# Deformable sampling in tiles of 6 by 16 pixels for 2 by 12 positions, with the corners out of reach gathered apart

## The chip, the core and the metric

The kernel runs on one core of one Trainium2 chip. The metric is device time in microseconds (us) of one execution; a kernel's time is the median of its runs. TensorE (PE in the profile, its weight loads PEld) multiplies matrices, VectorE (DVE) and ScalarE (ACT) work elementwise and carry results out of TensorE's accumulators, GpSimd (POOL) does small leftovers, SyncE (SP) issues most DMAs. Each engine works through its own instructions in order and waits on semaphores of the others.

## The reference

Two images of 256 channels and 128 by 128 pixels pass two layers. Layer 0 normalises by groups, runs three branches (dilation 1, 9, 12) of a deformable depthwise 3 by 3 convolution, and then a 1 by 1 convolution, three layer norms over channels and an MLP. Layer 1 is a group norm and a plain 3 by 3 convolution with quantised weights. What the change touches is the deformable part: each pixel and tap has its own offset, computed by a convolution, and the sample is bilinear between four corners.

```python
def _bilinear(x, py, px):
    y0, x0 = jnp.floor(py), jnp.floor(px)
    for dy in (0.0, 1.0):
        for dx in (0.0, 1.0):
            yc, xc = y0 + dy, x0 + dx
            wgt = (1.0 - jnp.abs(py - yc)) * (1.0 - jnp.abs(px - xc))
            valid = (yc >= 0) & (yc < H) & (xc >= 0) & (xc < W)
            ...
            out = out + g * (wgt * valid)[:, None]

def _branch(x, w_off, w_def, lw, lb, pad, dil):
    off = _conv(x, w_off, pad, dil)
    y = _deform_dw(x, off, w_def, pad, dil)
    return jax.nn.gelu(_ln2d(y, lw, lb), approximate=False)
...
x1 = _branch(x, off_w1, def_w1, bw1, bb1, 1, 1)
x2 = _branch(x, off_w2, def_w2, bw2, bb2, 9, 9)
x3 = _branch(x, off_w3, def_w3, bw3, bb3, 12, 12)
out = _ln2d(x1 + x2 + x3 + c, n1_w, n1_b)
h = gelu(h @ mlp_w1.T + mlp_b1) @ mlp_w2.T + mlp_b2
```

## The kernel before

**Phase A** (`phase_a`, once an image) normalises the image, writes it pixel by pixel into a table in DRAM (`table`, 256 channels a row), computes the offsets (`offsets`, eight image rows a call) and turns them into hat functions (`make_hats`): for each tap and each row or column of a tile, the weight `min(|distance|, 1) - 1` of every output pixel. They go to DRAM (`hats`). `offsets` keeps the largest absolute offset of its rows in `amax` (L381). After phase A the maximum over all of them goes through GpSimd into a flag (L512 to L518), and the program branches on it: above REACH, the general path `sample_any` gathers every corner; else `sample_near` runs, as it does here.

**The sampling stage** (`sample_near`) never gathers. A tile of the table, TR by TC = 8 by 16 pixels, lies on the 128 partitions (`xs`, L764). It serves RI by CI = 2 by 10 base positions, with a reach of 3 pixels on each side. For a unit (image, row of tiles, branch) `build` (L816) multiplies the row hats `hy` with the column hats `hx` into `A`, the bilinear weights of every pixel of a tile for every position and tap. A matmul of the tile with `A` (L889) is then the sampling of 2 x 10 positions x 9 taps = 180 columns; 14 tiles cover a row. ScalarE copies the result into `ev` (L898, three buffers); VectorE adds it, tap by tap, into a ring of image rows per branch (`accumulate`, L867; the first tap by ScalarE, L860). This is done for each of two channel halves: I call one unit's one half a c-step. There are 67 rows of tiles an image, so a row of tiles makes six c-steps and a group of four image rows twelve.

**The tail** (`Tail`) is the rest of layer 0, written as generators that `advance` steps along: at the head of each c-step, once in its middle, and elsewhere. `normalised` (L576) is a layer norm over channels: transposes of the pixels (L593) into PSUM, a copy to `T` (L595), statistics on VectorE (L603, L605), scale on ScalarE (L614), transposes back (L626). `branch` runs it on the ring's finished rows for each branch and group; `finish` adds the 1 by 1 convolution, the MLP and two more norms (L573, L682, L686, L720, L741). A branch's norm begins LAG = 5 advances after its rows are done.

The order on every engine in this stage is that of the program text, since the instructions are pinned (`pin`). In a c-step it is: the tail's pieces, the matmuls and copies (with the tail's middle piece), then, in the second half, `prepare(u + 2)`, which builds the unit after the next and so needs this unit's `A` free, and loads hats; then `accumulate`. `A` has two buffers, so the builds of a c-step stand on VectorE between its matmuls and its accumulation.

**Phase C** is layer 1's convolution.

Of the kernel before, what the change touches and what calls it, by code (L numbers as in the profile page):

```python
# [9 lines left out]
F32 = mybir.dt.float32  # L10
I32 = mybir.dt.int32
U32 = mybir.dt.uint32
BF16 = mybir.dt.bfloat16
# [6 lines left out]
P = 128  # L20
# [18 lines left out]

REACH = 3  # L40
LIMIT = float(REACH)
RI, CI = 2, 10
TR, TC = RI + 2 * REACH, CI + 2 * REACH
NT = -(-(W + 2 * REACH) // CI)
WT = NT * CI + 2 * REACH
AO = 12
WA = 28 + W
NH = TR + TC
HALF = 64
# [6 lines left out]
LAG = 5  # L56
XCLS = (0, 1, 2, 8, 9)
NPAT = RI + len(XCLS) + 1

# [8 lines left out]
def conv_preact_kernel(ctx: ExitStack, tc: tile.TileContext, t: dict, out: bass.AP):  # L68
# [66 lines left out]

    table = dram("table", [HT * WT, C])

    HY = H + 3
    hats = dram("hats", [NOFF // 6, TR + TC, HY, 3, W])
    offd = dram("offd", [H, W, NOFF])  # L140
    g12d = dram("g12d", [C, HW])
# [33 lines left out]
    gn1 = []  # L175
    amax = const.tile([P, NB * (H // ZG)], F32, name="amax")

# [99 lines left out]
    def phase_a(b, pool, psum, k, beside):  # L277
# [53 lines left out]
        def offsets(G):  # L331
# [37 lines left out]
            for br, dil in enumerate(DILS):  # L369
# [9 lines left out]
            nc.vector.tensor_copy(offs.rearrange("p r n -> p (r n)"), po[:, 0 : ZG * NOFF])  # L379
            i = b * (H // ZG) + G  # L380
            nc.vector.tensor_reduce(  # L381
                amax[:, i : i + 1],
                offs.rearrange("p r n -> p (r n)"),
                AX.X,
                ALU.max,
                apply_absolute_value=True,
            )
            nc.sync.dma_start(
# [3 lines left out]
            parts = k["parts"][G % 2]  # L392
            rest = pool.tile([P, ZG, NOFF], F32, name="rest", tag="rest", bufs=2)
            first, second = parts[:, 0, :, 0:NOFF], parts[:, 0, :, HALF : HALF + NOFF]
# [55 lines left out]
    with ExitStack() as actx:  # L450
        psum = actx.enter_context(tc.tile_pool(name="ps_a", bufs=1, space=PSUM))

        def gps():
# [7 lines left out]
            "wz": ap.tile([P, KC, NZ], F32, name="wz"),  # L461
            "shift": ap.tile([P, len(dxs), P], F32, name="shift"),
            "hatw": ap.tile([P, 2, NTAP * NH], BF16, name="hatw"),
            "parts": [ap.tile([P, 2, ZG, P], BF16, name=f"parts{i}") for i in range(2)],
# [8 lines left out]
        for b in range(NB):  # L473
            stats = ap.tile([P, KC, NGRP, 6], F32, name=f"stats1_{b}", tag=f"stats1_{b}")
            for c in range(KC):
                for g0 in range(0, NGRP, XT):
                    xt = ap.tile([P, XT * NG], F32, name="xt", tag="xt", bufs=3)
                    nc.sync.dma_start(
                        xt,
                        x[b, c * P : (c + 1) * P].rearrange("p h w -> p (h w)")[  # L480
                            :, g0 * NG : (g0 + XT) * NG
                        ],
                    )
                    for j in range(XT):
                        nc.vector.bn_stats(stats[:, c, g0 + j, :], xt[:, j * NG : (j + 1) * NG])
            if b == 0:
                load_now()
                nc.sync.dma_start(k["wz"], t["wz"].rearrange("(k p) n -> p k n", p=P))
                nc.sync.dma_start(k["shift"], t["shift"])
                hatw = ap.tile([P, 2, NTAP * NH], F32, name="hatw32", tag="xt", bufs=3)  # L490
                nc.sync.dma_start(hatw, t["hatw"])
                nc.vector.tensor_copy(k["hatw"], hatw)
                pattern = ap.tile([P, NG], F32, name="pattern", tag="xt", bufs=3)
                nc.sync.dma_start(pattern[HALF : HALF + NPAT], t["pattern"])
                for pl in k["planes"]:
                    nc.vector.tensor_copy(
                        pl[HALF : HALF + NPAT, 1, :], pattern[HALF : HALF + NPAT]
                    )
            mean, rstd = group_norm(stats, f"gn1_{b}", gps)
            gn1.append((mean, rstd))  # L500

            nc.vector.tensor_scalar(negmean[b], mean, -1.0, None, ALU.mult)
            for c in range(KC):
                nc.vector.tensor_scalar(
                    convs[b][:, c, :], convs[b][:, c, :], rstd[:, c : c + 1], None, ALU.mult
                )
            phase_a(b, ap, psum, k, beside)
# [3 lines left out]

    far = small.tile([P, 1], F32, name="far", tag="far")  # L512
    nc.vector.tensor_reduce(far, amax, AX.X, ALU.max)
    farall = small.tile([P, 1], F32, name="farall", tag="farall")
    nc.gpsimd.partition_all_reduce(farall, far, P, bass.bass_isa.ReduceOp.max)
    flag = const.tile([P, 1], I32, name="flag")
    nc.vector.tensor_scalar(flag, farall, LIMIT, None, ALU.is_gt)
    beyond = nc.values_load(flag[0:1, 0:1], min_val=0, max_val=1)  # L518
    same = nc.values_load(eq[0:1, 0:1], min_val=0, max_val=1)

# [4 lines left out]
    class Tail:  # L525
# [3 lines left out]

        def __init__(self, pool, psum, pin):  # L530
            self.pool, self.psum, self.pin = pool, psum, pin
            self.waiting, self.running = deque(), []
            self.now = self.last = self.norms = 0
            self.read = set()
# [41 lines left out]
        def normalised(self, z, src, what=None):  # L576
# [8 lines left out]
            T = self.tile("T")  # L585
            Tv = T.rearrange("p k n -> p (k n)").rearrange("p (j c) -> p j c", c=C)
            for h in range(NB4 // 2):
                tp = self.bank("tp")
                for j in range(2):
                    for c in range(KC):  # L590
                        i = j * KC + c
                        px = slice((2 * h + j) * P, (2 * h + j + 1) * P)
                        pin(nc.tensor.transpose(tp[:, i * P : (i + 1) * P], src[:, c, px], ident))  # L593
                pin(
                    nc.scalar.copy(  # L595
                        Tv[:, 2 * h : 2 * h + 2, :].rearrange("p j c -> p (j c)"), tp
                    )
                )
# [153 lines left out]
    def sample_near(pool, psum, k):  # L752

        pin = tc.keep_in_program_order
        tail = Tail(pool, psum, pin)
        units = [(b, Rt, br) for b in range(NB) for Rt in range(NR) for br in BRS]
# [3 lines left out]
        def load_tiles(b, Rt):  # L760

            xts[b, Rt] = []
            for T in range(NT):
                xt = pool.tile([P, C], F32, name="xs", tag="xs", bufs=20)  # L764
                src = bass.AP(
                    table[b].tensor,
                    table[b].offset + (Rt * RI * WT + T * CI) * C,
                    [[C, TC], [WT * C, TR], [1, C]],
                )
                nc.sync.dma_start(xt, src)  # L770
                xts[b, Rt].append(xt)
# [10 lines left out]
        def load_hats(u):  # L782
            b, Rt, br = units[u]
            for ky in taps(u):
                i0, i1 = valid(Rt, br, ky)
                hq = hats[b][br * 3 + ky + 1]
                y0 = Rt * RI - REACH - ky * DILS[br] + i0
                hy = pool.tile([P, RI, 3, W], F32, name="hy", tag="hy", bufs=3)
                hx = pool.tile([P, RI, 3, W], F32, name="hx", tag="hx", bufs=3)
                pitch = HY * 3 * W  # L790
# [78 lines left out]
        def sample(u, c):  # L869
# [13 lines left out]
            for T in range(0, NT, 2):  # L883
                if T // 2 == NT // 4:
                    tail.advance()
                pm = psum.tile([P, 2, 256], F32, name="pm", tag="pm", bufs=4)
                for j in range(2):
                    pin(
# [9 lines left out]
                    nc.scalar.copy(  # L898
                        ev[:, m0:m1, T * CI : (T + 2) * CI].rearrange(
                            "p m (t j) -> p t m j", j=CI  # L900
                        ),
                        pm[:, :, 0:n].rearrange("p t (m j) -> p t m j", j=CI),
                    )
# [36 lines left out]
    def sample_any(b, pool, psum):  # L940
        xbase = pool.tile([P, NTAP], F32, name="xbase", tag="xbase", bufs=1)
        nc.sync.dma_start(xbase, t["xbase"])
        dw = pool.tile([P, NTAP, C], F32, name="dw", tag="dw", bufs=1)
        nc.sync.dma_start(dw, t["defwt"].partition_broadcast(P))
        with tc.For_i(0, H, 1) as y:
            of = pool.tile([P, NOFF], F32, name="of", tag="of", bufs=1)
            nc.sync.dma_start(of, offd[b][bass.ds(y, 1)].rearrange("a w n -> w (a n)"))
            yb = pool.tile([P, NTAP], F32, name="yb", tag="yb", bufs=1)
            nc.sync.dma_start(
# [8 lines left out]
            for c, src in ((0, yb), (1, xbase)):  # L958
                nc.vector.tensor_tensor(
                    pos[:, c * NTAP : (c + 1) * NTAP].rearrange("p (b k) -> p b k", k=9),  # L960
                    ov[:, c],
                    src.rearrange("p (b k) -> p b k", k=9),
                    ALU.add,
# [13 lines left out]
            for dy, wy in ((0, om), (1, pos)):  # L977
                for dx, wx in ((0, om), (1, pos)):
# [5 lines left out]
                        xi, fl[:, NTAP : 2 * NTAP],  # L984
                        float((2 * REACH + dy) * WT + 2 * REACH + dx), None, ALU.add,
                    )
# [5 lines left out]
            for tap in range(NTAP):  # L992
                s = pool.tile([P, C], F32, name="s", tag="s", bufs=2)
                for j in range(4):
# [4 lines left out]
                        out_offset=None,  # L999
                        in_=table[b],  # L1000
                        in_offset=bass.IndirectOffsetOnAxis(ap=at[:, i : i + 1], axis=0),
# [33 lines left out]
    with cmp.Else():  # L1035
        with ExitStack() as bctx:
            psum = bctx.enter_context(tc.tile_pool(name="ps_b", bufs=1, space=PSUM))
            pool = bctx.enter_context(tc.tile_pool(name="bpool", bufs=1))
            k = {
                "A": [pool.tile([P, 9, RI, WA], F32, name=f"A{i}") for i in range(2)],  # L1040
            }
# [276 lines left out]
```

## Time and profile before

| what | us |
|---|---|
| median of three runs (7613.6 to 7631.05) | 7616.63 |
| the profiled execution, its own time | 7634.92 |
| its span in the profile | 7633.1 |
| TensorE busy | 7040.9 (92%) |
| VectorE busy | 6109.5 (80%) |
| ScalarE busy | 4832.0 (63%) |
| GpSimd busy | 712.8 (9%) |

Phase A ends at about 934 us, the first tiles of the sampling stage are asked for at 941.6, and phase C begins at about 6590. Inside the sampling stage each image starts with about ten rows of tiles without much tail work. An f32 matmul is recorded as two matmul instructions; a transpose or a bf16 matmul as one. The busy share of an engine is over the whole span; what sets the pace of the sampling stage is to be read from that stage alone, and from where one engine stands in its program relative to another.

### The profile page before, as it was taken

Reading aid. Unit: us, or ns where it says so; the run is one execution under the profiler, and the core shown is the slowest. Engines: PE = TensorE matmul, PEld = TensorE weight load, DVE = VectorE, ACT = ScalarE, POOL = GpSimd, SP = SyncE. Lnnn points to the kernel's source line nnn. Section 1 sums busy time; section 2 is a strip of 40 time slices with the busy share of each in tenths; the row PEclk is TensorE's granted clock in tenths of the full one; section 3 lists DMA queues with packets and bytes.
Section 4 is the critical chain, followed back from the end, with each engine's and each line's share of the span. In section 5 each row is a group of like instructions: output and inputs, shape, how many; then the busy total and the mean of one; then the engine's idle time right before and its main releaser. Section 6 shows DMA issues by size and latency. Waiting matters only on the chain. (4 is left out here: it accounts for less than half of the span.)

```text
span 7633.1 us, 114421 instructions
## 1 busy us (share of the span) xinstructions
PE 7040.9 (92%) x37984; PEld 5353.3 (70%) x37984; DVE 6109.5 (80%) x12723; ACT 4832.0 (63%) x10150; POOL 712.8 (9%) x1292
## 2 busy tenths in 40 slices
PE   6899888999999999999988999999999999899999
PEld 3555487777887788887777877887888777444444
DVE  7756557888888888988578888888888986677675
ACT  2344366777777777777676777777777777433232
POOL 0000000111111111111100111111111111000000
PEclk9999989999999999999999999999999999899999
DMA  8866689999999999998699999999999995222121
GB/s 285 265 193 197 181 231 250 248 253 256 256 255 252 254 259 255 258 256 231 180 239 246 254 255 253 256 254 253 251 259 254 254 252 161 90 75 76 69 78 47
DMA packets 856311, 1658.87 MB, mean 217 GB/s; under 512 B 116704, under 2 KB 403216, under 8 KB 851480
## 3 DMA queue, kind: packets, MB, share of 16 engines
q1 hardware_dynamic: 838296, 1617.84, 78.1%
q10 hardware_dynamic: 17408, 33.56, 1.3%
q8 instruction: 304, 4.98, 0.3%
q14 instruction: 303, 2.48, 0.1%
HBM read 1381.02 MB, written 270.06 MB: 216 GB/s over the span
## 5 line engine op out<-in xcount | busy, mean ns | idle before, releaser
L889 PE MATMUL pm<-A,xs 128*128 128x180 f32 (+2 forms) x22288 | 3624.6, 318 | 355.6 <-ACT ev L898 248.8
L889 PEld LDWEIGHTS pm<-A,xs 128*128 128x128 f32 x22288 | 3400.5, 195 | 598.0 <-ACT ev L898 347.0
L867 DVE SCALAR_TENSOR_TENSOR ring<-ev,defw,ring 128x256 f32<-128x256 f32 (+3 forms) x6344 | 2780.4, 459 | 339.1 <-ACT ev L898 159.0
L898 ACT COPY ev<-pm 128x360 f32<-128x360 f32 (+2 forms) x5572 | 2244.9, 449 | 791.3 <-PE pm L889 483.3
L816 DVE TENSOR_TENSOR A<-hy,hx 128x768 f32<-128x768 f32 x1130 | 1026.1, 947 | 413.1 <-DMA hx<-hats 300.6
L1172 PE MATMUL pc<-cring,signs 128*128 128x512 bf16 x4608 | 1005.3, 381 | 20.0 <-ACT cring L1119 13.3
L1172 PEld LDWEIGHTS <-signs 128*128 128x128 bf16 x4608 | 452.0, 98 | 572.8 <-issue 27.0
L614 ACT ACTIVATE T<-T,rs 128x256 f32<-128x256 f32 x1280 | 661.9, 589 | 180.5 <-POOL rs L610 180.4
L607 POOL TENSOR_SCALAR rs<-mv 128x4 f32<-128x4 f32 x320 | 122.8, 384 | 4904.3 <-DVE mv L605 2681.5
L573 PE MATMUL hp<-T,w 128*128 128x512 f32 x1024 | 503.8, 617 | 12.9 <-ACT T L692 12.9
L603 DVE BATCH_NORM_STATS2 st<-T 128x6 f32<-128x256 f32 x1280 | 447.0, 412 | 25.3 <-ACT T L595 25.2
L320 PE MATMUL pz<-wz,xa 128*128 128x486 f32 x1024 | 463.7, 582 | 3.1 <-DVE zr L327 3.1
L573 PE MATMUL h<-hT,w 128*128 128x512 f32 x1024 | 460.1, 592 | 0.0
L642 ACT ACTIVATE T<-zc,bb,bw 128x512 f32<-128x512 f32 x384 | 277.5, 773 | 228.0 <-PE zc L626 227.9
L860 ACT ACTIVATE ring<-ev,defw 128x256 f32<-128x256 f32 (+1 forms) x788 | 392.2, 503 | 24.1
L1180 ACT ACTIVATE o<-xl,l1b 128x1024 f32<-128x1024 f32 x64 | 73.5, 1148 | 501.8 <-DMA out_x<-o 394.8
L626 PEld LDWEIGHTS zc<-ident,T 128*128 128x128 f32 x2560 | 315.0, 147 | 96.3 <-issue 61.9
L626 PE MATMUL zc<-ident,T 128*128 128x128 f32 x2560 | 358.7, 284 | 19.7 <-ACT T L614 13.8
L595 ACT COPY T<-tp 128x512 f32<-128x512 f32 x640 | 340.5, 583 | 42.5 <-PE tp L593 42.3
L609 POOL TENSOR_TENSOR rs<-rs,mhalf 128x4 f32<-128x4 f32 x320 | 365.0, 1141 | 0.0
L1119 ACT CAST cring<-D 128x2048 bf16<-128x2048 f32 (+1 forms) x140 | 245.0, 1755 | 183.4 <-PE pc L1172 125.1
L573 PEld LDWEIGHTS h<-hT,w 128*128 128x128 f32 x1024 | 189.1, 190 | 186.6 <-issue 186.1
(118 smaller groups left out, 5226.4 us busy)
## 6 DMA issues: line engine op xcount, KB each, us to landing
hy<-hats SPq DMA_DIRECT2D x1114, 384.0 KB
hx<-hats SPq DMA_DIRECT2D x1114, 384.0 KB
xs<-table SPq DMA_DIRECT2D x1876, 128.0 KB
g12d<-T SPq DMA_DIRECT2D x128, 512.0 KB
other<-g12d SPq DMA_DIRECT2D x128, 512.0 KB
hats<-hb SPq DMA_DIRECT2D x64, 720.0 KB
hats<-hb SPq DMA_DIRECT2D x64, 576.0 KB
xl<-x1d SPq DMA_DIRECT2D x56, 640.0 KB
```

The lines of the kernel that those rows point to most:

```text
L320: nc.tensor.matmul(pz[:, 0:NZ], lhsT=xt[:, c, r, :], rhs=k["wz"][:, c, :], start=c == 0, stop=c == KC - 1,)
L573: nc.tensor.matmul(out, lhsT=w, rhs=v, start=i == 0, stop=i == n - 1)
L603: pin(nc.vector.bn_stats(st[:, j, :], Tv[:, j, :]))
L609: nc.gpsimd.tensor_tensor(rs[:, 0, :], rs[:, 0, :], mhalf[:, 0:NB4], ALU.pow)
L614: nc.scalar.activation(Tv[:, j, :], Tv[:, j, :], AF.Identity, scale=rs[:, 0, j : j + 1], bias=rs[:, 1, j : j + 1],)
L626: nc.tensor.transpose(zc[:, j * P : (j + 1) * P], Tv[:, j, c * P : (c + 1) * P], ident)
L816: nc.vector.tensor_tensor(dst, hy[:, i0:i1].rearrange("p i t w -> p t i w"), hx[:, i0:i1].rearrange("p i t w -> p t i w"), ALU.mult,)
L860: pin(nc.scalar.mul(dst, src, w))
L867: pin(nc.vector.scalar_tensor_tensor(dst, src, w, dst, ALU.mult, ALU.add))
L889: nc.tensor.matmul(pm[:, j, 0:n], lhsT=xts[b, Rt][T + j][:, c * P : (c + 1) * P], rhs=A[:, m0:m1, AO + (T + j) * CI : AO + (T + j + 1) * C ...
L898: nc.scalar.copy(ev[:, m0:m1, T * CI : (T + 2) * CI].rearrange("p m (t j) -> p t m j", j=CI), pm[:, :, 0:n].rearrange("p t (m j) -> p t m ...
L1172: nc.tensor.matmul(pc[:, bank, :], lhsT=w[:, m * P : (m + 1) * P], rhs=xc[:, i, k, t * JC : (t + 1) * JC, kx : kx + W], start=j == 0, stop ...
```

## The change

The reach falls from 3 pixels to 2, and tiles of 6 by 16 pixels (96 partitions) serve 2 by 12 positions. Eleven tiles cover a row, a matmul has 216 columns, and there are 66 rows of tiles an image. `xs` has 18 buffers for 20. Hats keep their number of rows in DRAM.

`offsets` no longer keeps one maximum: for every pixel it keeps, per component, the largest distance of an offset from the middle of its tile's reach (`reach`). After phase A, `missing` lists the pixels where that is over what a tile covers, up to 42 of them, by counting and small matmuls, reads their offsets and base positions back with indirect DMAs, and works out for up to two taps a pixel the weights and table rows of the corners that no tile has. `lacking` gathers those rows and sums them into `extra` [126, 3 branches, 256 channels], each value split into three bf16 parts on three partitions. The flag now says that the lists overflow.

In the tail, `normalised`, when called from `branch`, makes a selection matrix `S` on VectorE (1 where a list entry's pixel is a column's pixel) and adds `S` times `extra` to the transposes in PSUM, with two bf16 matmuls a bank.

```diff
-REACH = 3
-LIMIT = float(REACH)
-RI, CI = 2, 10
+REACH = 2
+RI, CI = 2, 12
...
+PX = TR * TC
...
+SLOTS = 42
+ROWS = 3 * SLOTS
+EACH = 2
...
-            nc.vector.tensor_reduce(
-                amax[:, i : i + 1],
-                offs.rearrange("p r n -> p (r n)"),
-                AX.X,
-                ALU.max,
-                apply_absolute_value=True,
-            )
+            rest = pool.tile([P, ZG, NOFF], F32, name="rest", tag="rest", bufs=2)
+            nc.vector.tensor_tensor(rest, offs, k["mid"], ALU.subtract)
+            planes = rest.rearrange("p r (b c k) -> p c r b k", c=2, k=9)
+            for comp in range(2):
+                nc.vector.tensor_reduce(
+                    reach[:, comp, b * H + G * ZG : b * H + (G + 1) * ZG],
+                    planes[:, comp], AX.XY, ALU.max, apply_absolute_value=True,
+                )
...
+    def missing(psum, pool):
...
+        nc.vector.tensor_scalar(V, reach[:, 0], SPAN[0], None, ALU.is_gt)
+        nc.vector.scalar_tensor_tensor(V, reach[:, 1], SPAN[1], V, ALU.is_gt, ALU.max)
+        nc.vector.tensor_reduce(cnt, V, AX.X, ALU.add)
...
+        gather(of, offs_all, 0)
+        gather(base[:, 0], t["ybase"], 1)
+        gather(base[:, 1], t["xbase"], 2)
...
+    def lacking(pool, m):
...
+                m["gather"](G, tables, i, m["idx"][:, j])
...
+        miss = missing(ps_m, mpool)
+    extra, ids = lacking(mpool, miss), miss["ids"]
     farall = small.tile([P, 1], F32, name="farall", tag="farall")
-    nc.gpsimd.partition_all_reduce(farall, far, P, bass.bass_isa.ReduceOp.max)
+    nc.gpsimd.partition_all_reduce(farall, miss["worst"], P, bass.bass_isa.ReduceOp.max)
...
+            add = what is not None and self.offs is not None
+            if add:
+                b, br, g = what
+                S = pool.tile([ROWS, NG], BF16, name="S", tag="S", bufs=2)
+                pin(
+                    nc.vector.tensor_scalar(
+                        S, self.offs, float((b * NGRP + g) * NG), ids, ALU.add, ALU.is_equal
+                    )
+                )
             for h in range(NB4 // 2):
                 tp = self.bank("tp")
                 for j in range(2):
                     for c in range(KC):
                         i = j * KC + c
                         px = slice((2 * h + j) * P, (2 * h + j + 1) * P)
-                        pin(nc.tensor.transpose(tp[:, i * P : (i + 1) * P], src[:, c, px], ident))
+                        pin(
+                            nc.tensor.matmul(
+                                tp[:, i * P : (i + 1) * P], lhsT=src[:, c, px], rhs=ident,
+                                is_transpose=True, start=i == 0,
+                                stop=not add and i == 2 * KC - 1,
+                            )
+                        )
+                for j in range(2 if add else 0):
+                    px = slice((2 * h + j) * P, (2 * h + j + 1) * P)
+                    pin(
+                        nc.tensor.matmul(
+                            tp[:, j * C : (j + 1) * C], lhsT=S[:, px], rhs=extra[:, br, :],
+                            start=False, stop=j == 1,
+                        )
+                    )
...
-                xt = pool.tile([P, C], F32, name="xs", tag="xs", bufs=20)
+                xt = pool.tile([PX, C], F32, name="xs", tag="xs", bufs=18)
...
-                hy = pool.tile([P, RI, 3, W], F32, name="hy", tag="hy", bufs=3)
-                hx = pool.tile([P, RI, 3, W], F32, name="hx", tag="hx", bufs=3)
+                hy = pool.tile([PX, RI, 3, W], F32, name="hy", tag="hy", bufs=3)
+                hx = pool.tile([PX, RI, 3, W], F32, name="hx", tag="hx", bufs=3)
```

## The prediction

> **What bounds the kernel now.** I read the page's groups first, then the busy time by stage, then the timeline of one group of four rows. In the group rows the number after "|" is busy time in us and mean ns of one; after the second "|" comes the idle time before it and what ended it.
>
> ```profile
> L889 PE MATMUL pm<-A,xs 128*128 128x180 f32 (+2 forms) x22288 | 3624.6, 318 | 355.6 <-ACT ev L898 248.8
> L867 DVE SCALAR_TENSOR_TENSOR ring<-ev,defw,ring 128x256 f32<-128x256 f32 (+3 forms) x6344 | 2780.4, 459 | 339.1 <-ACT ev L898 159.0
> L816 DVE TENSOR_TENSOR A<-hy,hx 128x768 f32<-128x768 f32 x1130 | 1026.1, 947 | 413.1 <-DMA hx<-hats 300.6
> ```
>
> The sampling stage runs from about 942 to 6560 us. By stages (window and its length, then busy us of PE, weight loads, DVE, ACT, POOL with counts, granted clock, DMA share, GB/s):
>
> ```profile
> 958.00:1400.00 442.00, 373.02 (x2278) 351.06 (x2279) 321.89 (x681) 289.64 (x701) 23.12 (x44) 0.89 0.91 240
> 1400.00:3400.00 2000.00, 1902.07 (x10806) 1612.26 (x10805) 1783.89 (x4019) 1533.21 (x3364) 269.05 (x472) 0.99 0.97 255
> ```
>
> In the steady stretch TensorE is busy 95%, VectorE 89%, the DMA engines 97%: three resources are near their end at once. What lets them be so is that TensorE runs ahead. The timeline of both engines (start, us, engine, line):
>
> ```profile
> 2383.05 1.04 PE L593 MATMUL tp<-ident,ring 128*128 128x128 f32 x8
> ...
> 2398.15 2.61 PE L889 MATMUL pm<-A,xs 128*128 128x180 f32 x16
> ...
> 2402.31 1.04 PE L593 MATMUL tp<-ident,ring 128*128 128x128 f32 x8
> ```
>
> ```profile
> 2388.26 3.75 DVE L867 SCALAR_TENSOR_TENSOR ring<-ev,defw,ring 128x256 f32<-128x256 f32 x8
> 2391.92 1.82 DVE L816 TENSOR_TENSOR A<-hy,hx 128x768 f32<-128x768 f32 x2
> 2394.89 0.96 DVE L816 TENSOR_TENSOR A<-hy,hx 128x768 f32<-128x768 f32 x1 [1.15 <-DMA hx<-hats]
> 2395.77 3.77 DVE L867 SCALAR_TENSOR_TENSOR ring<-ev,defw,ring 128x256 f32<-128x256 f32 x8
> 2399.45 1.40 DVE L603 BATCH_NORM_STATS2 st<-T 128x6 f32<-128x256 f32 x4
> ...
> 2413.09 1.40 DVE L603 BATCH_NORM_STATS2 st<-T 128x6 f32<-128x256 f32 x4
> ```
>
> The transposes at 2383.05 and 2402.31 belong to the statistics at 2399.45 and 2413.09. VectorE comes to that place in its program 16.4 and 10.8 us after TensorE; over all 192 branch normalisations (3 branches x 64 groups) the mean of such pairs is 12.4 us. Now nobody minds: these transposes read rows finished long ago. One group of four rows takes 84.9 us (branch transposes at 1947.84, 2034.13, 2118.31 ... 2457.49), of which VectorE works 1783.9/2000 x 84.9 = 75.7 us.
>
> The last view is the clock beside a stall:
>
> ```profile
> 4031.65 8.61 PE L889 MATMUL pm<-A,xs 128*128 128x180 f32 x42 [6.31 <-DVE A L816]
> ```
>
> ```profile
> 4020.00:4025.30 5.30, 5.30 (x35) 5.06 (x34) 4.03 (x7) 4.45 (x11) 0.00 (x0) 1.00 1.05 249
> 4031.70:4035.60 3.90, 3.90 (x13) 3.90 (x14) 3.70 (x9) 0.33 (x1) 0.00 (x0) 0.50 1.03 246
> ```
>
> After 6.31 us without work TensorE runs at half clock for about 4 us: 300 ns for one matmul instruction, 151 before.
>
> **What the Trainium skill says.** "TensorE: Matmul & The Clock Gate", "Part 1: The HAM clock gate": an idle window of about 3.4 us halves the clock, and about 3.4 busy us restore it; the trace agrees (6.31 us idle, then 0.50). The same page, "Step-by-step: what each phase is for": matmuls stay in program order, and only weight loads are pulled ahead; so a matmul that waits holds all behind it. No row of this trace shows one held for a VectorE result made just before, but nothing contradicts it. The same page, "LDWEIGHTS (loading the stationary operand)": load time follows the columns, not the rows; the trace has 132 ns for 72x120 and 134 for 128x120, so 96 rows for 128 buy no TensorE time. "DMA: Bandwidth & Descriptors", "Anatomy of one DMA — SWDGE (gpsimd) path": about 2 us fixed for one DMA; no gather runs in this trace.
>
> **The change, part by part.**
> *Sampling matmuls.* A c-step (one unit, one channel half) has 14 matmuls of 180 columns, 28 instructions at 0.152 us (16 against 12 of them: 2.61 against 2.00 us) = 4.27 us. After: 11 of 216, 22 x 0.152 x 216/180 = 4.0 us. Twelve c-steps a group: -3.2 us of TensorE, if TensorE is the bound.
> *Evacuation.* ScalarE copies 7 x 464 ns become 5 of 432 elements and one of 216, about 5 x 520 + 350 ns: shorter, and beside the matmuls.
> *DMA.* hy and hx fall from 384 to 288 KB, xs from 14 x 128 to 11 x 96 KB: per row of tiles 8.7 MB become 6.2. VectorE's wait for hx was 300 us: 70 in 1400 to 3400 and as much in the second image's like stretch, so some 160 at the two image starts, where no tail work shares the time. I take 100 us back there, 0 to 160 as ends; the steady part is in the table below.
> *Accumulation and build* keep their instructions (6372 for 6344; 1124 for 1130) and durations, since they go by elements, not rows.
> *Phase A.* Per 8 rows one subtraction (0.60) and two reductions of 216 elements (about 0.38 each) for one reduction of 0.60: 24 us of VectorE in 32 groups, mostly under TensorE, busy 793 of 934 us: +8, 0 to 24. Eighteen fewer zero stores an image: nothing, they lie beside the loads.
> *Listing the pixels.* In the built order the new section's first VectorE instruction comes after phase A's last, and the branch after its last. About 150 VectorE instructions, mostly 0.16 to 0.2 us, some of 0.9 (35 us); nine small matmuls with their round trips (7); three gathers, then ten (5 and 12). Sum 59, of which a little hides behind the 8 us in which hats stores land today: +55, ends 40 and 100.
> *The correction on the transposes.* Each branch normalisation gets S on VectorE (512 elements, 0.6 us) and four bf16 matmuls of 256 columns, about 0.11 us each. That is 1.8 and 1.3 us a group, not the point. The point is the wait. S stands on VectorE behind the accumulation of the c-step before, and every later TensorE instruction stands behind the matmul that needs S. So 192 times TensorE's lead is given up, and VectorE then waits until TensorE has made a whole c-step.
>
> I work out one group from its order after the change: S1 before steps 1 and 2, S2 before 3 and 4, S3 before 5 to 12. Blocks, from the timeline: accumulation 3.72, build of three 2.6, statistics 1.6, sampling matmuls of a step 4.0, one 512-column f32 matmul 0.86 (eight instructions, so four matmuls, in 3.60), eight transposes 0.87. Half clock after each stall costs TensorE 1.8 us (about 3.5 us at half speed); ends 0 and 3.4.
> From S1: step 1 with one w1 pair ends on TensorE at 6.6 + 1.8 = 8.4; its accumulation runs 8.9 to 12.6. Step 2, behind another w1 pair and with four w2 matmuls inside, ends at 17.6. The build must wait for that (A is in use): 17.7 to 20.3; accumulation, the second MLP sum (0.75) and S2 (0.6) end at 25.5. From S2: step 3 ends 6.7, accumulation 7.2 to 10.9, step 4 ends 11.6, then build, accumulation and S3: 18.8. From S3: step 5 is ready at 8.1; statistics of the finishing chain to 8.8; from then VectorE has hardly a gap: 8 accumulations 29.8, 4 builds 10.4, statistics 1.6, tail sums 2.7 + 2.8 + 1.2, S 0.6, and some 0.8 of waiting before the first build: 58.7. Sum 103 against 84.9: +18.1 us a group, 6.0 us an S. VectorE's waits for hx (3.0 us a group now) are gone in it, since it waits for TensorE instead. The S of the image starts and of the last flush, about 20 of 192, meet less of a lead; at half the price: 172 x 6.0 + 20 x 3.0 = +1092 us.
> Phase C stays.
> Sum against the profiled execution's span: 7633 + 1092 - 100 + 55 + 8 = 8688 us. That execution took 7634.9 by its own time, 18 over the median 7616.6, so 8670; the table lets every stall cost the clock, and the wait at S2 (4.0 us) is at the edge of that, 32 or so of 64 groups without it: -1.8 x 32 = -58. I say **8610 us**.
>
> **The rivals.**
> *A, the lead is lost, but cheaply.* The clock is kept, and VectorE's waits after S are filled by tail work in part: 103 less 5.4 (clock) and about 5 gives 92.6 us a group, +7.7 x 64 = +493; 7617 + 493 + 63 - 100 = about 8070. For: tail work is uneven. Against: the three waits in the table are 4 to 13 us long.
> *B, not slower: relief at the builds.* The DMA engines at 97% are what really sets the pace; with a quarter less traffic hx is there at L816, TensorE saves 3.2 us a group, and VectorE needs 75.7 + 1.8 + about 4 = 81.5: 7617 - 64 x 3.4 - 100 + 63 = about 7360. It decides if VectorE's lag at the branch transposes falls under some 2 us; accumulation and build alone are 6.3, so I hold it unlikely.
> *C, worse.* The order adds ScalarE's and POOL's waits to every restart and the clock stays halved longer: 6 to 12 us more a group, about 9000 to 9400. Upper end, a lag of 12.4 us paid in full each time and VectorE idle as long again for the refill: about 10000.
> *D, the change doesn't do what it says:* too many pixels are out of reach and the general path runs, several times longer. Offsets worked out from the reference's inputs put 12 pixels out of reach, two at most in a column, one tap each: far under 42.
>
> **How the numbers follow.** Forecast 0.56 (own range 8300 to 8900), A 0.22 (7900 to 8300), C 0.14, B 0.06, D 0.01, no change 0.01. With B and the lower part of A left out below and the upper half of C above, the range is 7950 to 9050. What a measurement can tell from no change is 0.2%, 15 us. Faster 0.06, same 0.02, slower 0.92.
>
> **What would show it.** The branch transposes' correction matmul waits for VectorE's S, 4 us and more, some 192 times; TensorE's busy share of the steady stretch falls from 95% to near 75%, and the granted clock from 0.99 to about 0.9; the DMA share falls to near 65%; the hx wait nearly goes; a group takes about 102 us; some 55 us more lie between phase A and sampling. I am wrong if the correction matmuls find S ready, or if a group takes under 85 us.

## The result, and the profile after

The changed kernel takes 8840.89 us (median of 4 runs, 8839.17 to 8842.32) against 7618.01 for the kernel before: ratio 1.160, 95% interval 1.158 to 1.162. The profiled execution has a span of 8837.3 us against 7633.1, so 1204 us are to be found. The first sampling matmul starts at 988.1 us where it was 958.2: 30 us. The sampling stage up to phase C's group norm grows from 5630 to 6803 us: 1173. Phase C has the remaining 1 us.

The costliest groups of the changed kernel's page (busy time, mean ns of one, then idle time before and what ended it):

```profile
L1140 PE MATMUL pm<-A,xs 96*128 96x216 f32 (+2 forms) x17424 | 3572.7, 362 | 226.9 <-ACT ev L1149 161.8
...
L1117 DVE SCALAR_TENSOR_TENSOR ring<-ev,defw,ring 128x256 f32<-128x256 f32 (+4 forms) x6372 | 2766.2, 457 | 988.4 <-ACT ev L1149 794.4
...
L837 PE MATMUL tp<-extra,S 126*128 126x256 bf16 x768 | 231.3, 403 | 1200.7 <-DVE S L817 1200.7
...
L1066 DVE TENSOR_TENSOR A<-hy,hx 96x768 f32<-96x768 f32 (+1 forms) x1124 | 1004.0, 944 | 150.8 <-PE pm L1140 114.8
```

The third row is new: TensorE stands 1200.7 us ahead of the correction's matmuls, and VectorE's selection matrix `S`, which I call the mask from here on, ends all of it: 6.25 us for each of 192 masks. The second row is the other half: VectorE's accumulations, once 339.1 us late, are 988.4 us late, behind ScalarE's copies of matmuls that TensorE had not yet made. VectorE's waits at the builds fall from 413.1 to 150.8 us.

The same two stretches as before, by windows (same columns):

```profile
958.00:1400.00 442.00, 317.33 (x1707) 300.34 (x1708) 316.91 (x665) 242.74 (x578) 22.77 (x42) 0.81 0.62 171
1400.00:3400.00 2000.00, 1583.18 (x7380) 1316.77 (x7379) 1440.29 (x3228) 1165.38 (x2445) 186.71 (x372) 0.89 0.54 153
```

TensorE falls from 95 to 79% busy, VectorE from 89 to 72%, the DMA engines from 97 to 54%, the granted clock from 0.99 to 0.89: nothing is near its end any more, and each waits for the other. From the starts of the branch transposes a steady group of four rows takes 107.5 us, before 84.9. One group on TensorE (start, us, engine, line; in brackets the idle time before):

```profile
2455.70 0.60 PE L828 MATMUL tp<-ident,ring 128*128 128x128 f32 x4
2465.80 0.61 PE L837 MATMUL tp<-extra,S 126*128 126x256 bf16 x2 [9.50 <-DVE S L817]
...
2487.70 0.60 PE L828 MATMUL tp<-ident,ring 128*128 128x128 f32 x4
2491.98 0.61 PE L837 MATMUL tp<-extra,S 126*128 126x256 bf16 x2 [3.67 <-DVE S L817]
...
2504.01 0.60 PE L828 MATMUL tp<-ident,ring 128*128 128x128 f32 x4
2511.03 0.61 PE L837 MATMUL tp<-extra,S 126*128 126x256 bf16 x2 [6.41 <-DVE S L817]
```

and on VectorE, around the first of the three:

```profile
2451.79 6.84 DVE L1117 SCALAR_TENSOR_TENSOR ring<-ev,defw,ring 128x236 f32<-128x236 f32 x14
2458.55 2.69 DVE L1066 TENSOR_TENSOR A<-hy,hx 96x768 f32<-96x768 f32 x3
2461.16 4.19 DVE L1117 SCALAR_TENSOR_TENSOR ring<-ev,defw,ring 128x256 f32<-128x256 f32 x8
2465.26 0.48 DVE L817 TENSOR_SCALAR S<-offs_n,ids 126x512 bf16<-126x512 f32 x1
...
2475.73 3.80 DVE L1117 SCALAR_TENSOR_TENSOR ring<-ev,defw,ring 128x256 f32<-128x256 f32 x8 [6.35 <-ACT ev L1149]
```

TensorE has its transposes done at 2456.3 and can go no further. VectorE first finishes accumulations and a build that stand ahead of `S`; the mask itself takes 0.48 us. Then it is VectorE's turn to wait: its next accumulation finds no sampled columns until 2475.73. That is the lead of TensorE given up, three times a group.

### The profile page after: what moved, and what is told of

Its sections match the earlier page's. It is cut to its first block, busy times and chain, and to the rows that moved or that the text cites. A ratio compares the mean times of both kernels' runs of the same rounds, so it can differ in the third digit from the quotient of the medians.

```text
span 8837.3 us, 104978 instructions
## 1 busy us (share of the span) xinstructions
PE 7200.0 (81%) x33906; PEld 5410.0 (61%) x33906; DVE 6268.9 (71%) x13147; ACT 4662.1 (53%) x9398; POOL 657.0 (7%) x1305
## 5 line engine op out<-in xcount | busy, mean ns | idle before, releaser
L1140 PE MATMUL pm<-A,xs 96*128 96x216 f32 (+2 forms) x17424 | 3572.7, 362 | 226.9 <-ACT ev L1149 161.8
L1140 PEld LDWEIGHTS pm<-A,xs 96*128 96x128 f32 x17424 | 3284.7, 207 | 505.3 <-ACT ev L1149 276.3
L1117 DVE SCALAR_TENSOR_TENSOR ring<-ev,defw,ring 128x256 f32<-128x256 f32 (+4 forms) x6372 | 2766.2, 457 | 988.4 <-ACT ev L1149 794.4
L1149 ACT COPY ev<-pm 128x432 f32<-128x432 f32 (+2 forms) x4752 | 2008.5, 473 | 857.7 <-PE pm L1140 813.5
L837 PE MATMUL tp<-extra,S 126*128 126x256 bf16 x768 | 231.3, 403 | 1200.7 <-DVE S L817 1200.7
L843 ACT COPY T<-tp 128x512 f32<-128x512 f32 x640 | 362.3, 588 | 1553.6 <-PE tp L837 1519.9
L1066 DVE TENSOR_TENSOR A<-hy,hx 96x768 f32<-96x768 f32 (+1 forms) x1124 | 1004.0, 944 | 150.8 <-PE pm L1140 114.8
L851 DVE BATCH_NORM_STATS2 st<-T 128x6 f32<-128x256 f32 x1280 | 467.3, 416 | 550.2 <-ACT T L843 549.9
L837 PEld LDWEIGHTS <-S 126*128 126x128 bf16 x768 | 81.3, 128 | 1257.1 <-DVE S L817 1245.8
L798 PE MATMUL hp<-T,w 128*128 128x512 f32 x1024 | 482.8, 594 | 0.9 <-ACT T L940 0.9
```

Source lines behind the costliest of these rows:

```text
L798: nc.tensor.matmul(out, lhsT=w, rhs=v, start=i == 0, stop=i == n - 1)
L851: pin(nc.vector.bn_stats(st[:, j, :], Tv[:, j, :]))
L1066: nc.vector.tensor_tensor(dst, hy[:, i0:i1].rearrange("p i t w -> p t i w"), hx[:, i0:i1].rearrange("p i t w -> p t i w"), ALU.mult,)
L1117: pin(nc.vector.scalar_tensor_tensor(dst, src, w, dst, ALU.mult, ALU.add))
L1140: nc.tensor.matmul(pm[:, j, 0:n], lhsT=xts[b, Rt][T + j][:, c * P : (c + 1) * P], rhs=A[:, m0:m1, AO + (T + j) * CI : AO + (T + j + 1) * C ...
L1149: nc.scalar.copy(ev[:, m0:m1, T * CI : (T + nt) * CI].rearrange("p m (t j) -> p t m j", j=CI), pm[:, 0:nt, 0:n].rearrange("p t (m j) -> p ...
```

## The experiments

| run | what differs from the change | us | ratio to before (95%) | steady group, us |
|---|---|---|---|---|
| e1_s_early | mask made five advances earlier | 7672.77 | 1.007 (1.005 to 1.010) | 87.3 |
| e2_no_fix | no correction in the tail | 7687.66 | 1.009 (1.006 to 1.011) | 87.9 |
| e3_old_tiles_late | tiles of before | 9217.81 | 1.210 (1.207 to 1.212) | 112.7 |
| e4_warm | idle matmuls fill the wait | 8535.23 | 1.120 (1.118 to 1.123) | 100.4 |
| e5_xs22 | mask early, 22 tile buffers | 7672.53 | 1.005 (1.003 to 1.006) | 87.5 |
| e6_xn_pool | mask early, `xn` loaded by GpSimd | 7282.36 | 0.954 (0.951 to 0.956) | 80.0 |
| e7_old_tiles_early | mask early, tiles of before | 7750.64 | 1.015 (1.013 to 1.018) | 85.9 |
| e8_before_xn_pool | kernel before, `xn` loaded by GpSimd | 7623.10 | 1.000 (0.998 to 1.001) | 84.4 |
| e9_no_fix_xn_pool | no correction, `xn` loaded by GpSimd | 7193.98 | 0.944 (0.942 to 0.946) | 78.7 |
| e10_mask_pool | mask late but on GpSimd, `xn` loaded by GpSimd | 7337.03 | 0.963 (0.961 to 0.964) | 80.4 |

The steady group is worked out from the starts of the branch transposes between 1400 and 2200 us; the kernel before has 84.9, the change 107.5.

**Is it the wait? e1 and e2.** In e1 the same mask is made when the branch is put into the tail's queue, five advances earlier, with eight buffers:

```diff
+        def select(self, what):
+            if what not in self.made:
+                b, br, g = what
+                S = self.pool.tile([ROWS, NG], BF16, name="S", tag="S", bufs=8)
+                self.pin(nc.vector.tensor_scalar(S, self.offs, float((b * NGRP + g) * NG), ids, ALU.add, ALU.is_equal))
+                self.made[what] = S
+            return self.made[what]
-        def begin(self, chain, wait):
+        def begin(self, chain, wait, what=None):
+            if what is not None and len(self.made) < 8 - 1:
+                self.select(what)
...
-                S = pool.tile([ROWS, NG], BF16, name="S", tag="S", bufs=2)
-                pin(nc.vector.tensor_scalar(...))
+                S = self.select(what)
+                del self.made[what]
```

> The change as it is, but S is written on VectorE when a branch's norm is queued (five tail advances, two and a half c-steps, before the transposes use it) and not right before them; S has eight buffers. Same matmuls, same work. If the wait for S carries the loss: TensorE's 1201 us of idle before the correction matmuls falls under 100 us, the clock goes back to 0.97, a group of four rows takes 80 to 84 us (107.6 in the changed kernel) and the time is 7150 to 7400 us. If the narrower tiles, the longer matmuls or the correction's own work set the pace, it stays over 8500.

In e2 `add = what is not None and self.offs is not None` becomes `add = False`.

> Leaves out the correction: no S and no correction matmuls, so the 12 listed pixels lack their far corners; the listing and gathering between phase A and the sampling stage stay. If only the wait matters, it equals the version with S made early, less the correction's own work, 92 us of VectorE and some 84 us of TensorE at the most: 7050 to 7300 us. If the matmuls of the correction cost beyond their wait, it is 200 us or more below that version.

Measured: 7672.77 and 7687.66 us. In e1 TensorE's wait for the mask is 28.7 us, where it was 1200.7:

```profile
L848 PE MATMUL tp<-extra,S 126*128 126x256 bf16 x768 | 150.1, 277 | 28.7 <-DVE S L767 28.7
```

The loss is gone with the wait, whether the mask is made early or not at all: 1168 us by moving one instruction of 0.48 us. But both lie above the ranges that were expected (7150 to 7400 and 7050 to 7300). Smaller tiles, with DMA at 67% where it was 97%, should have left the kernel faster than before, and it was not. The windows of e1 show TensorE at 91% and a clock of 0.96, so something still stopped it:

```profile
1400.00:3400.00 2000.00, 1820.15 (x9053) 1501.99 (x9052) 1753.37 (x3984) 1427.65 (x3002) 253.20 (x460) 0.96 0.67 189
```

Its timelines of TensorE, of ScalarE and of SP name it, once in each group:

```profile
2081.91 6.67 PE L813 MATMUL pc<-xn,convw 128*128 128x512 f32 x8 [5.65 <-ACT xn L924]
```

```profile
2081.13 1.33 ACT L924 ACTIVATE xn<-xn,negmean 128x512 f32<-128x512 f32 x2 [5.27 <-DMA xn<-in_x]
```

```profile
2061.86 4.47 SPq L1031 DMA_DIRECT2D xs<-tables  x6
2066.38 0.58 SPq L912 DMA_DIRECT2D other<-g12d  x1
2067.05 1.85 SPq L1031 DMA_DIRECT2D xs<-tables  x3
...
2073.17 1.18 SPq L1031 DMA_DIRECT2D xs<-tables  x2
2074.44 0.54 SPq L920 DMA_DIRECT2D xn<-in_x  x1
```

The 1 by 1 convolution's input `xn` is asked for at 2074.44 and used at 2081.13, 6.7 us later; ScalarE waits 5.27 us for it, TensorE 5.65, and then the eight matmuls run 6.67 us where eight of this shape take 3.70 at full clock. On SP's queue `xn` stands behind eleven tile loads and six loads of hats (left out at the dots), which SP issues one after the other from 2061.86 on. e2 has the same stall, 369.9 us over its whole run where e1 has 283.1, so it is no faster than e1 though it does less. In the kernel before it is issued 26 to 29 us ahead and directly behind `other`, as here at 2496.57:

```profile
2495.41 0.47 SPq L653 DMA_DIRECT2D other<-g12d  x1
2496.57 0.37 SPq L661 DMA_DIRECT2D xn<-in_x  x1
```

The DMAs of SP are not pinned to the program text, so the edit moved them without saying so; the changed kernel with its late mask still has `xn` 31 to 33 us ahead. Rival: VectorE at 88% is simply the bound.

**Which of the two: e5, e6, and the control e8.** e5 is e1 with `bufs=22` for `xs` and 6 for `S`; e6 is e1 with one word changed; e8 is that word in the kernel before.

```diff
-            nc.sync.dma_start(xn, x[b]...)
+            nc.gpsimd.dma_start(xn, x[b]...)
```

> The mask early as in the run with the mask early (7672.77 us), and the sampling tiles get 22 buffers in place of 18 (two rows of 11), the masks 6 in place of 8; nothing else changes. Theory X: with the wait for the mask gone, the time is held up by a new stall on SP's queue: the load of xn stands there behind loads of sampling tiles, which wait until TensorE has read the buffers that they are to fill; it is issued 6.5 us ahead of its use where it was 27 us in the kernel before, lands late, and TensorE waits 5.3 us once in each group of four rows, then runs its convolution at half clock. Whole, that is 283 us of waiting and some 55 us of clock. With 22 buffers no tile load waits for matmuls of its own row, xn is issued more than 10 us ahead, the stall goes: 7330 to 7500 us. Rival Y: VectorE, 88 % busy, is what bounds the steady stretch (its own work is 77 us of a group of 87), and the smaller tiles have nothing to give there: 7600 to 7700 us, with TensorE's wait for xn replaced by waits of the same sum elsewhere.

> The mask early, 18 buffers for sampling tiles as in the change, and only the load of xn moved from SP's queue to GpSimd's. Theory X (xn stands behind tile loads on SP's queue): the load no longer waits for the matmuls that free tile buffers; GpSimd is 9 % busy and its waits are short, so the stall of 5.3 us in each group goes and the time is 7330 to 7500 us, near the run with 22 buffers. Rival Y (VectorE bounds): 7600 to 7700 us. Rival Z: the stall comes not from the place on the queue but from a late free buffer for xn; then xn is still issued some 6 us ahead of its use and the time stays at 7670.

> The kernel before, with only the load of xn moved from SP's queue to GpSimd's. There xn is issued 27 us ahead of its use and nothing waits for it, so under theory X (the move undoes a stall that came only with the new queue order) nothing changes: 7590 to 7660 us. Rival W: the move is a gain of its own on any version, for instance because SP's queue becomes shorter; then 7350 to 7550, and the 390 us of the run with the mask early and the load moved are not the tiles' work.

e5 changed nothing, 7672.53 us. Its `xn` is still issued 6.2 to 7.6 us ahead, SP's waits for matmuls at tile loads are 232 us in 1400 to 3400 against 275, and the order of the queue is the same. So the part of the theory that named the number of buffers is wrong: more room for tiles doesn't bring `xn` forward, and the loads ahead of it stay. e6 took the load off that queue and gave 7282.36 us, 390 less than e1, under the low end of what was expected: the waits and the clock had been counted as 283 and 55 us, and the other 52 were not traced. There `xn` is issued 9.4 to 11.4 us ahead, and nothing waits long for it. Who waited for `xn` in e1, and below it in e6 (us, times, over 1400 to 3400):

```profile
  DVE T L941: 140.0, 45
  PEld pc L813: 130.5, 23
  PE pc L813: 122.8, 23
  ACT xn L924: 116.4, 23
```

```profile
  PEld pc L813: 20.6, 50
  PE pc L813: 3.3, 12
```

```profile
1400.00:3400.00 2000.00, 1930.21 (x9971) 1618.01 (x9970) 1904.86 (x4341) 1559.00 (x3299) 308.82 (x529) 1.00 0.75 206
```

The last line is e6's window: clock 1.00, TensorE 96%, VectorE 95%, DMA 75%. Now VectorE is near its end, which in e1 it was not: the rival falls. e8 gave the ratio 1.000, so the move has no gain of its own where `xn` was in time.

**What do the tiles bring, and what does the correction cost? e3, e7, e9.** For e3 and e7:

```diff
-REACH = 2
-RI, CI = 2, 12
+REACH = 3
+RI, CI = 2, 10
...
-NH = TR + TC + 2
+NH = TR + TC
-XCLS = (0, 1, 3, 9, 11)
+XCLS = (0, 1, 2, 8, 9)
...
-                xt = pool.tile([PX, C], F32, name="xs", tag="xs", bufs=18)
+                xt = pool.tile([PX, C], F32, name="xs", tag="xs", bufs=20)
```

e7 has e1's edit besides, with six buffers for the mask. e9 has `add = False` as in e2, and `xn` on GpSimd's queue.

> The tiles of before (reach 3, 8 by 16 pixels for 2 by 10 positions, 20 xs buffers) with the changed kernel's listing and its correction, S made right before its use. No pixel is then out of reach, so the correction adds zeros, at the same cost. If the wait is what costs, it costs the same here: about 8841 plus 64 x 3 to 7 us for the longer matmuls and the DMA: 9000 to 9250 us. If the new tiles cause the loss, it is near 7620 + 120 = 7740 us.

> The tiles of before (2 by 10 positions, reach 3) with the listing and the correction, and the mask made early; so what the correction costs without its wait, on the old tiles. Where the tiles save on TensorE only and xn is the reason that this was not seen: 7660 to 7780 us (before, plus 38 us of listing and phase A, plus 192 masks of 0.48 us and their matmuls of 0.11 us, plus some of the waits of a full DMA). If it is under 7640 us, the smaller tiles bring nothing or harm once the wait is gone, stall or not. If it is over 7900 us, a wait for the mask is still in it.

> The tiles and the listing without the correction (no mask, no matmuls of it; pixels whose corners lie out of reach are left without them), and the load of xn on GpSimd's queue. Against 7282.36 us with the correction and the mask early. If VectorE bounds the steady stretch now (95 % busy in the run with mask early and load moved), the 192 masks of 0.48 us come off whole: 92 us, so 7170 to 7220. If TensorE's small stalls share the bound, half of it: 7220 to 7260. If the mask is hidden once it is early: 7265 to 7300.

With the late mask the tiles of before take 9217.81 us, with the early mask 7750.64: the wait costs 1467 us there, so it needs no small tile. In e7 `xn` is issued 26 to 30 us ahead, so that stall is absent from e7 as from e6. The wait for the mask is small in e7 but not gone:

```profile
L848 PE MATMUL tp<-extra,S 126*128 126x256 bf16 x768 | 151.0, 278 | 104.1 <-DVE S L767 103.9
```

In e6 it is 31.3 us. The two differ by 468 us, so the tiles' own worth is between 395 and 468, if the 73 us more of waiting count at most in full. Of the 468, 283 lie in 48 steady groups, the 5th to the 28th of each image (5.9 us a group), and the rest mainly at the starts and ends of the images. e9 against e6 is the price of the correction once hardly anything waits for it: 88 us, near the 92 us that 192 masks of 0.48 us keep VectorE busy, as expected where VectorE sets the pace. On the old tiles the listing and the correction together cost 7750.64 - 7633.01 = 117.6 us against the kernel before in its own call; in e7's profile 48 of them lie ahead of the first sampling matmul (1006.1 us where it was 958.2).

**What does the clock cost? e4.** The change with dummy bf16 matmuls on the identity, put where TensorE would stand; nothing reads their results:

```diff
+                for _ in range((14, 26, 40)[br] if add and h == 0 else 0):
+                    pin(nc.tensor.matmul(tp, lhsT=ident_b, rhs=warm, start=True, stop=True))
```

> The change with idle matmuls (bf16, 512 columns of ones into the bank that the transposes then overwrite) on TensorE before each branch's transposes: 14, 26 or 40 of them for branch 1, 2, 3, at 0.215 us each 3.0, 5.6 and 8.6 us, a little under the stalls measured there (3.7, 6.4, 9.5). They only keep the clock up. If half clock after the stalls costs 1.8 to 3 us an S, the granted clock is above 0.96 and the time 8841 - 192 x 2.2 = about 8420 us (8270 to 8500). If the clock plays no part, it is 8841 or a little more.

```profile
1400.00:3400.00 2000.00, 1891.59 (x9436) 1445.31 (x9495) 1542.49 (x3466) 1249.89 (x2620) 201.76 (x400) 1.00 0.58 165
```

8535.23 us at a clock of 1.00: half clock after the stalls costs some 306 us of the change's loss, 1.6 us for each mask. The result lies 35 us above the range that was expected. The dummies may delay transposes whose wait was shorter than they are; whether that is the 35 us was not tried.

**VectorE's queue, or the place in the program? e10.** The mask stays at its late place; `nc.vector.tensor_scalar` becomes `nc.gpsimd.tensor_scalar`, and `xn` is loaded as in e6.

> The mask stays at its late place in the program, at the transposes, and is made by GpSimd and not by VectorE; the load of xn goes on GpSimd's queue too. If the loss of 1170 us is the mask's place behind VectorE's queued accumulations, and not its late place in the program as such, then GpSimd, whose queue has only short steps, makes it long ahead of TensorE, and VectorE is spared 92 us: 7190 to 7330 us. Rival: GpSimd makes it late as well, since it stands in order behind the scales of a normalisation that waits for VectorE, or the two disturb each other: 7400 to 8000 us, with waits for S in TensorE's groups.

7337.03 us, just over its range. GpSimd takes 2.18 us where VectorE takes 0.48:

```profile
L817 POOL TENSOR_SCALAR S<-offs_n,ids 126x512 bf16<-126x512 f32 x75 | 163.6, 2181 | 6.8
```

and yet TensorE waits only 6.2 us for it at its matmuls in 2000. The mask needs nothing that is late; it was late because of what stood ahead of it on VectorE. That e10 doesn't gain the 92 us that VectorE is spared goes with slower accumulations: the forms of 256, 236 and 242 elements take 488, 478 and 495 ns, 480, 464 and 471 in e6. The trace shows where: between 1400 and 3400 us the 288 of them that run beside a mask take 771, 548 and 551 ns, and the others 480, 464 and 471 as in e6. That is 29 us in the 2000, where VectorE is spared 36. Of the 55 us between e10 and e6, 16 lie in the 48 steady groups and the rest outside them; TensorE's whole wait for the mask is 76.4 us in e10 and 31.3 in e6.

## Why the prediction was right, and where it was off

The forecast was 8610 us with its reason, and the measured 8840.89 lies 231 us above it. By its steps:

*The place of the loss: right.* TensorE's lead over VectorE is given up at every mask, 192 times. e1 removes the loss by the mask's place in the program alone; e10 removes it with the mask at its late place, by its queue (and, as e6, has `xn` in time). The prediction says that no row of the trace before shows a matmul held for a VectorE result; its own row at 4031.65 shows one, 6.31 us for `A`.

*The group, worked out by hand: right in its form, 4.5 us short.* Measured from the timeline:

| stretch | predicted, us | measured, us |
|---|---|---|
| S1 to S2 | 25.5 | 26.2 |
| S2 to S3 | 18.8 | 19.05 |
| S3 to the next S1 | 58.7 | about 62 |
| group | 103 | 107.5 |

Most of the miss is in the third stretch: step 5 is ready 10.2 us after the end of the mask and not 8.1, and several of its accumulations have 10 or 11 instructions, where the sum had blocks of eight.

*Half clock, 1.8 us a stall: right in size (1.6 by e4); the 58 us taken off for S2 were wrong.* The wait at S2 of 3.67 us goes with half clock too, as it does in 46 of the 48 steady groups. The windows after S1, a little later, after S2, and at the end of the stage after a gap of 2.79 us:

```profile
2466.00:2470.00 4.00, 4.00 (x15) 3.68 (x14) 1.79 (x8) 1.69 (x3) 0.39 (x2) 0.50 0.41 110
2472.00:2476.00 4.00, 4.00 (x17) 2.80 (x16) 0.27 (x1) 2.51 (x6) 0.00 (x0) 1.00 0.00 0
```

```profile
2492.00:2495.00 3.00, 3.00 (x12) 2.74 (x13) 1.23 (x4) 1.17 (x2) 0.00 (x0) 0.50 1.02 268
```

```profile
7667.00:7669.50 2.50, 2.50 (x13) 2.38 (x12) 0.94 (x3) 1.26 (x3) 1.31 (x3) 0.50 0.00 0
```

*100 us taken back at the image starts: not seen, because the first masks take it.* The transposes of the third branch of the first group come 221.8 us after sampling begins, where they came 229.5 before: 8 us. By the start of the third group the change is 4 us behind the kernel before, and from the 31st group of the first image to the third of the second it gains 5. The wait for hx did go (27.6 us by form, 300.0 before), and in e1, with the mask early, these two stretches are 41 and 70 us shorter than in the kernel before. So the relief is there, and about as large as the sum had it. What failed is the half price for the masks at the starts: of the first six masks of each image, eleven of the twelve stop TensorE for 6.5 to 14.8 us, more than the mean of 6.25, and the clock in 958 to 1400 is 0.81.

*Listing and phase A, +55 and +8: too much.* Together 30 us by the first sampling matmul. The first gather of the listing is issued at 936.1 us, about where phase A ended before, and the last at 964.5, so a good part of the listing's 59 us of steps must lie beside phase A's end; step by step that was not followed. In the experiments with the same listing the first sampling matmul comes 28 (e4) to 56 us (e5) later than in the kernel before, all under the 63 of the sum.

So against the predicted span (8630 us, before the step to the median): 33 us less ahead of sampling, and 239 more in it. Counted from the starts of the branch transposes, the 48 steady groups cost 1084 us more than before, where the sum had 825 (18.1 us each, less their share of the 58). All the rest of the sampling stage cost 90, where it had 109. So the term that was too small is the steady group: 22.6 us more than before, priced at 18.1, and at some 17.2 after the 58. That the rest came out near is luck: relief and dear masks at the image starts lie in it together with cheap masks at the end of the first image, where the last ten stop TensorE for 0.4 to 4.7 us.

*Sampling matmuls, -3.2 us a group: visible only without stalls, and then larger.* e7 to e6 is 5.9 us a group. VectorE waits for hx 83.3 us between 1400 and 3400 in e7 and not at all in e6, which is 3.6 us a group; TensorE's rest of waiting for the mask in e7 is another 1.6 at most. The change itself could not show it.

*Rival B* (about 7360 us, 81.5 a group) held that a lighter DMA and TensorE would make it not slower. The kernel as changed isn't that, but e6 with 80.0 us a group is: its price was sound, its condition, that `S` be found ready, failed. *Rival A* (92.6 a group with the clock kept) was too low: e4 keeps the clock and still takes 100.4. *C's* numbers began at 9000 and were not reached. The price of the wait was put at 6.0 us a mask against the old group; against the same tiles without stalls it is (8840.89 - 7282.36) / 192 = 8.1 us, part of which is the tiles' own gain, unseen.

Open is why SP's order moved `xn` behind the loads of tiles and hats in e1, e2 and e5 and not in the change or in e7.

## What to carry to other kernels

An instruction that needs nothing late becomes late by its place on an in-order queue; where one engine runs ahead of another, make the small operands of the leading engine well before it gets there, or on a queue that is not behind. After a stall is removed, compare again how far ahead each load is issued, since the queue of DMAs may have been reordered by the edit: the second stall here, 390 us, hid the gain of the smaller tiles. A control with only the last fix in the old kernel tells whose gain it was.

## What the runs showed of the hardware

- Half clock came sooner than expected. The Trainium skill, "TensorE: Matmul & The Clock Gate", Part 1, speaks of an idle window of about 3.4 us; here a gap of 2.79 us was followed by a clock of 0.50, after other short gaps. This is one case; the window is not shown to be shorter.
- The Trainium skill, "GPSIMD Engine Reference", 4.1 Engine selection, calls one-input elementwise work on GpSimd roughly as fast as the line rate. Here the mask, one tensor with a scalar a partition, took 2.18 us against 0.48 on VectorE; the measurement decides. It is no wait for VectorE: three masks during which VectorE did nothing took 2.01 us. The same page, "1. Specifications", says that VectorE's instructions with two inputs in SBUF contend with GpSimd. The trace of e10 agrees: accumulations, which have two, took 548 to 771 ns on average beside a mask and 464 to 480 without one, the longest 1.31 us. Over all of them that is 8 to 24 ns each.
- A DMA issued by GpSimd holds it for 0.79 us, and `xn` landed 4.5 to 6.8 us after issue in e6; with an issue some 10 us ahead of use this is enough.
